# A four-layer transformer block on one core: gates cut into pieces, a context copy moved, and loads tied behind a point of the order

## The chip, the cores and the metric

The kernel runs on one core of one Trainium2 chip. The metric is the device time of one execution, in microseconds. The kernel before takes 3809.88 us, the median of three runs (3807.89 to 3815.07). The profile comes from one further execution, which took 3822.21 us.

## The reference

Eight sequences of 512 tokens by 256 features, with a context of the same shape for each, go through four residual steps. All arithmetic that matters here is in 32-bit floats.

```python
x = x + tanh(g_xattn[0]) * mlstm(layernorm(x), ctx, ctx)     # "cell": 8 heads of 32
x = x + tanh(g_ffn[0])   * attn_and_experts(layernorm(x))    # 32 heads of 8, then experts
x = x + tanh(g_xattn[1]) * cross_attention(ctx, ctx, layernorm(x))  # 16 heads of 16
x = x + tanh(g_ffn[1])   * product_key_experts(layernorm(x)) # top 8 of 4096
```

The part that the change is about is the first line's gates. From query, key and value a small product makes 8 input gates and 8 forget gates for each token. Then, along the 512 tokens of a sequence:

```python
log_f = log_sigmoid(fg)
cs = cumsum(log_f, axis=1)
log_D = cs[:, :, None] - cs[:, None, :] + ig[:, None, :]     # masked above the diagonal
D_mat = exp(log_D - max(log_D, axis=-1))
C = (q k^T / sqrt(32)) * D_mat
h = (C / (max(|sum C|, exp(-max log_D)) + 1e-6)) v
```

The kernel needs of it, for each head and token, the running sum cs and the running maximum of (input gate - cs). Both are scans along the tokens.

## The kernel before, in words

The program has two stages. The attention phase (to about 2850 us of the profile) does the first three residual steps for all sequences. The final stage (L1459 on) does the product-key experts. The change touches only the attention phase.

**The main loop.** Attention is cut into 24 jobs. A job is one sequence's 16 heads: ("A", m, 0) and ("A", m, 1) are the two halves of the self-attention of the m-th sequence in order, ("C", m, 0) is its cross-attention. Each job has 16 steps, and a step has two halves. A job passes through the loop twice. First its maxima: per half step 8 matrix instructions make scores of 128 queries by two heads by 512 keys in PSUM (`sc`, two buffers, L422), and VectorE reduces them to negative maxima (`nm`, L440). Later its exponentials: the scores are made again with the maximum folded in, and ScalarE takes the exponential (`pr`, L469), which then multiplies the values (`av`, L485). In the steady state each half step holds one product of maxima of one job and one product of exponentials of an earlier job. A job starts its maxima when its operands are there (`ready`). If it isn't ready, the loop goes on with the exponentials alone.

**Lanes beside it.** Everything else in the phase is written as Python generators, called lanes, which are stepped between the half steps: `between` (moves operands of A jobs), `values1`, `after`, `before((0, 2, ... 7))` (cell and queries of the sequences but the second), `behind` (experts, then the operands of C jobs), `before((1,))` (cell and queries of the second sequence, in buffers lent by the experts), `contexts` (keys and values of the cross-attention) and `fill` (products for the final stage). A lane yields a number, the TensorE time that it has just used; or ("wait", t), after which it isn't stepped until a nominal clock has advanced by t; or ("rest", event), after which it is stepped once the event has been noted; or ("take", ...), for a PSUM bank. In each half step `beside` (L1353) hands out a credit of TensorE time. It goes through the lanes in a fixed order of preference and steps the first that can run. The two lanes at places 3 and 4 (cells; experts) change places with each turn. Once the first job has begun, the lane of the second sequence stands ahead of both.

**Who sets the order on an engine.** TensorE executes in the order in which the program is traced (`manual_schedule` with PE alone, L1448). On the other engines a planner orders the instructions by its own costs and by their readiness, and it may move an instruction that is ready far ahead of where it was traced. `tc.issue_after(ins)` ties the instructions traced in its block that are on `ins`'s engine behind `ins` in that engine's order. `beside` uses it: VectorE instructions of a lane's step stay behind the newest reduction of maxima.

**The gates.** In `cell` (L713), after the product `gp` (L726), VectorE adds the gates' biases (L735, two instructions on 8 partitions by 512 tokens). ScalarE takes Abs, Exp and Ln (L742 to L744; the last needs another table). VectorE then makes log_sigmoid (L745), the running sum (L746, a scan), the difference (L750), the running maximum (L752, a scan), their sum (L753) and a sign (L754). The result goes to DRAM, from where it is broadcast to all partitions. All of this is traced in one step of the lane.

**The start.** The first sequence's x (`x0`), the gates' weights, its transposed context (`cT0`) and its context (`cx0`) are loaded first. `load_keys` copies the context into a spread layout `cte` (L228, on ScalarE for the first sequence, on GpSimd for later ones). The first cell's weighed sums (L693) read `cte`. After the first cell come the queries: keys and queries are stored to DRAM and loaded back in another layout (`spread`), values (`vk`, L946 and L948) are stored by GpSimd's queue (L953). Then the first job's maxima can begin. `pk` and `vk` share two buffers.

**Loads on GpSimd's queue.** `load` (L526, a sequence's x for the experts), `load_context` (L532), `Tiles.begin` (L565, x and context of the cells from the third sequence on) and the reload of x at L882 are issued from GpSimd. Weights of the experts are too, and do not change. Nothing but readiness ties the former to a place in GpSimd's order.

Of the kernel before, what the change touches and what calls it, by code (L numbers as in the profile page):

```python
# [10 lines left out]
F32 = mybir.dt.float32  # L11
# [4 lines left out]
AF = mybir.ActivationFunctionType  # L16
# [20 lines left out]
def kernel(  # L37
# [142 lines left out]
    def attention_phase(ctx: ExitStack):  # L180
# [39 lines left out]
        cte = cst.tile([P, NC, WC], F32, name="cte")  # L220
        nc.vector.memset(cte, 1.0)

        def load_keys(eng, staged, ce, b, copy):

            eng.dma_start(staged, cx[b].rearrange("(c p) d -> p c d", p=P))
            for c2 in range(2):
                part = slice(2 * c2, 2 * c2 + 2)
                copy(  # L228
                    ce[:, part, : 8 * 33].rearrange("p c (h e) -> p c h e", e=33)[:, :, :, 0:32],
                    staged[:, part].rearrange("p c (h e) -> p c h e", e=32),  # L230
                )

        load_keys(
            nc.sync, trp.tile([P, NC, D], F32, name="cx0", tag="Xa"), cte, order[0], nc.scalar.copy
        )

        gwm = cst.tile([P, 4, 40], F32, name="gwm")
        nc.gpsimd.memset(gwm, 0.0)
# [284 lines left out]
        kds, vcs = {}, {}  # L523
        xbs, lnx, qks, vds, xds, weights = {}, {}, {}, {}, {}, {}

        def load(m):  # L526

            xbs[m] = xbp.tile([P, NC, D + 1], F32, name="X")
            nc.gpsimd.dma_start(xbs[m][:, :, :D], xds[m])
            nc.gpsimd.memset(xbs[m][:, :, D], 1.0)  # L530

        def load_context(m, tag):  # L532
            cT = cxp.tile([P, NK, S], F32, name="cT", tag=tag)
            nc.gpsimd.dma_start(cT, cxT[order[m]].rearrange("(k p) s -> p k s", p=P))
            return cT

        def load_first(n):
# [17 lines left out]
        class Tiles:  # L555
# [9 lines left out]
            def begin(self, m):  # L565

                b = order[m]
                if m == 0:
                    return x0, cT0, cte
                qn = self.tokens("qn")  # L570
                self.loader.dma_start(qn, x[b].rearrange("(c p) d -> p c d", p=P))
                cT, ce = self.context(m)
                load_keys(self.loader, self.stream(), ce, b, nc.gpsimd.tensor_copy)
                return qn, cT, ce

            def context(self, m):
# [136 lines left out]
        def cell(m, own, loaded):  # L713
# [24 lines left out]
            if m == 0:  # L738
                with tc.issue_after(gated.ins):
                    constants()  # L740

            nc.scalar.activation(e, z, AF.Abs)  # L742
            nc.scalar.activation(e, e, AF.Exp, scale=-1.0)
            nc.scalar.activation(e, e, AF.Ln, bias=1.0)  # L744
            nc.vector.scalar_tensor_tensor(z, z, 0.0, e, ALU.min, ALU.subtract)  # L745
            nc.vector.tensor_tensor_scan(  # L746
                cs, ones[:8, 0:1].to_broadcast([8, S]), z, 0.0, ALU.mult, ALU.add
            )

            nc.vector.tensor_tensor(a, a, cs, ALU.subtract)  # L750
            nM = z
            nc.vector.tensor_tensor_scan(nM, a, a, -3.0e38, ALU.max, ALU.max)  # L752
            nc.vector.tensor_tensor(cs, cs, nM, ALU.add)  # L753
            nc.vector.tensor_scalar(nM, nM, -1.0, None, ALU.mult)  # L754
            nM_d = drm.tile([8, S], F32, name="nM_d")
# [123 lines left out]
                if pair == 2:  # L879
                    rested.add(("cell", m))  # L880
            Xa = own.stream()
            nc.gpsimd.dma_start(Xa, x[b].rearrange("(c p) d -> p c d", p=P))  # L882
            if m == 0:
                mu, rs = yield from layernorm(None, hk, "q")
                for c in range(NC):
# [16 lines left out]


        def queries(m, own, Xa):
            xn = own.tokens("xn")


# [34 lines left out]
            for c in range(NC):  # L942
                ps = project(w, nT, c)
                pk = trp.tile([P, S], F32, name="vk", tag="pk", bufs=2)[:, : 32 * 9]
                heads = pk.rearrange("p (h e) -> p h e", e=9)
                nc.gpsimd.memset(heads[:, :, 8], 1.0)  # L946
                for f in range(2):
                    nc.any.tensor_copy(  # L948
                        heads[:, 16 * f : 16 * f + 16, 0:8].rearrange("p (j g) e -> p j g e", g=4),
                        ps.rearrange("p (j f g e) -> p j f g e", f=2, g=4, e=8)[:, :, f],  # L950
                    )

                (nc.sync if m else nc.gpsimd).dma_start(  # L953
                    vds[m][:, :, c], pk.rearrange("p (f n) -> p f n", f=2)
                )
                yield 1.0
# [103 lines left out]
        def contexts():  # L1060

            for half in (range(M // 2), range(M // 2, M)):
                for i in (1, 2):
                    if i == 1 and half[0]:
                        yield ("rest", ("A", 1, 0))
                    w = wsp.tile([P, NK, D], F32, name="wkv", tag="wkv")
                    nc.sync.dma_start(w, w3[i].rearrange("(k p) n -> p k n", p=P))
                    for m in half:
                        cT = load_context(m, "cT")
                        if m == 0 and i == 1:  # L1070
                            yield ("rest", ("begun", 0))
                        yield ("wait", 5)
                        for cost in (keys3, values3)[i - 1](m, w, cT):
                            yield cost
                            yield ("wait", 2)
# [277 lines left out]
        def beside(credit):  # L1353

            nonlocal turn
            while credit > 0:
                turn += 1
                first = lanes[:3] + (lanes[3:5] if turn % 2 else lanes[4:2:-1]) + lanes[5:]
                if ("begun", 0) in rested:
                    first.insert(3, lanes[5])  # L1360
                lane = next((lane for lane in first if lane.runnable()), None)
# [571 lines left out]
```

## Time and profile before

| | before |
|---|---|
| median of three runs | 3809.88 us (3807.89 to 3815.07) |
| profiled execution | 3822.21 us |
| its span, first to last instruction | 3820.4 us |
| PE busy | 3521.1 us, 92% |
| DVE busy | 2246.6 us, 59% |
| ACT busy | 1756.5 us, 46% |
| POOL busy | 600.5 us, 16% |
| mean granted TensorE clock | 0.968 |
| mean DMA traffic | 90 GB/s |

PE is TensorE's matmuls, PEld its weight loads, DVE VectorE, ACT ScalarE, POOL GpSimd, SP SyncE; a "q" behind a name is that engine's queue of DMA issues and waits. L440 is line 440 of the kernel. A group's row gives line, engine, operation and tile as out<-in. In a timeline the two numbers ahead of a row are its start and its busy time, both in us; in brackets stands how long the engine was idle before it and what ended that idleness. "x2" behind a row means that two instructions are merged in it. The row of digits of an engine in the page shows its busy tenths in 40 equal slices of the span, 95.5 us each; PEclk is the granted TensorE clock in tenths of full speed. Of the time around the span, 1.8 us, the profile tells nothing.

### The profile page before, as it was taken

How to read it: one execution, taken by the hardware profiler on the slowest of the kernel's cores; microseconds unless marked ns; L12 is line 12 of the kernel's file. 1: busy time of each engine (PE TensorE's matmuls, PEld its weight loads, DVE VectorE, ACT ScalarE, POOL GpSimd, SP SyncE). 2: the span in 40 equal slices, each digit the busy share in tenths (PEclk: the TensorE clock that was granted, in tenths of full speed). 3: DMA queues.
4: the chain of work that ended last, by engine and by line, in shares of the span. 5: the costliest groups of instructions: out<-in, count | busy, mean ns of one | idle time of the engine just before them, and what ended most of it. 6: DMA issues, size and time to landing. Idle time of an engine off the chain costs nothing.

```text
span 3820.4 us, 76232 instructions
## 1 busy us (share of the span) xinstructions
PE 3521.1 (92%) x31049; PEld 1833.6 (48%) x31049; DVE 2246.6 (59%) x5491; ACT 1756.5 (46%) x2300; POOL 600.5 (16%) x646
## 2 busy tenths in 40 slices
PE   5789888999999999999999999999899999999998
PEld 2333333443444344334433443434346777777777
DVE  4565656556555555545555543544422689999993
ACT  2124454444445444445445444444443455555552
POOL 3122102111101010101200200100000133333331
PEclk7779999999999999999999999999999999999999
DMA  4423212322412332332332242230434433333331
GB/s 128 114 72 85 66 48 79 90 72 63 123 53 81 92 87 80 90 90 68 96 93 59 80 109 87 90 85 23 139 118 149 119 110 107 107 107 107 107 106 38
DMA packets 225195, 345.35 MB, mean 90 GB/s; under 512 B 25982, under 2 KB 173470, under 8 KB 216542
## 3 DMA queue, kind: packets, MB, share of 16 engines
q1 hardware_dynamic: 206796, 277.43, 24.6%
q0 software_dynamic: 16864, 62.46, 5.6%
q8 instruction: 244, 4.00, 0.4%
q10 hardware_dynamic: 1184, 0.58, 0.1%
q14 instruction: 107, 0.88, 0.1%
HBM read 238.50 MB, written 101.09 MB: 89 GB/s over the span
## 4 chain that ended last, share of the span: by engine, by line
PE 78%; DVE 10%; ACT 2%; issue 2%; DMA 1%; POOL 0%; SPq 0%; DVEq 0%; ACTq 0%; POOLq 0%
PE sc L422 22%; PE acc L1775 12%; PE ps_hd L131 10%; PE av L485 7%; DVE nm L440 7%; PE cf L1755 4%; PE ps_y L1039 3%; PE ps_sim L1507 3%; PE ps_q L381 3%; PE ps_h L1020 3%; PE ps_p L370 2%; PE cav L842 2%; PE csc L857 2%; PE ps_hl L131 1%; PE ps_t L351 1%
## 5 line engine op out<-in xcount | busy, mean ns | idle before, releaser
L440 DVE TENSOR_REDUCE nm<-sc 128x2 f32<-128x1024 f32 x768 | 938.9, 1225 | 953.6 <-PE sc L422 952.3
L469 ACT ACTIVATE pr<-sc 128x1024 f32<-128x1024 f32 x768 | 783.0, 1023 | 949.9 <-PE sc L422 949.3
L422 PE MATMUL sc<-ka,qa 32*128 32x512 f32 x3072 | 913.0, 661 | 117.7 <-DVE nm L440 117.3
L422 PE MATMUL sc<-qa,ka 32*128 32x512 f32 x3072 | 864.9, 651 | 20.8 <-ACT pr L469 19.0
L1775 PE MATMUL acc<-up_sb,gs 64*128 64x256 f32 x4096 | 468.4, 382 | 1.3 <-DVE gs L1764 1.3
L422 PEld LDWEIGHTS sc<-ka,qa 32*128 32x128 f32 x3072 | 247.0, 187 | 462.4 <-DVE nm L440 275.0
L131 PE MATMUL ps_hd<-xT,dw 128*64 128x256 f32 x3584 | 432.8, 387 | 15.0 <-DVE pd L862 6.5
L485 PE MATMUL av<-pr,v 128*32 128x512 f32 x3072 | 420.9, 621 | 4.4 <-DMA v<-v_d 4.3
L1775 PEld LDWEIGHTS acc<-up_sb,gs 64*128 64x128 f32 x4096 | 390.0, 187 | 52.4 <-issue 4.7
L131 PEld LDWEIGHTS ps_hd<-xT,dw 128*64 128x64 f32 x3584 | 247.0, 138 | 231.4 <-issue 98.1
L1745 POOL TENSOR_TENSOR m<-o,cwT 128x1024 f32<-128x1024 bf16 x128 | 243.6, 1903 | 584.0 <-DVE o L1743 260.8
L1222 ACT COPY hb<-ps_hd 128x512 f32<-128x512 f32 x224 | 130.9, 585 | 286.3 <-PE ps_hd L131 250.9
L422 PEld LDWEIGHTS sc<-qa,ka 32*128 32x128 f32 x3072 | 233.1, 185 | 59.8 <-ACT pr L469 45.4
L485 PEld LDWEIGHTS av<-pr,v 128*32 128x32 f32 x3072 | 61.1, 109 | 301.6 <-issue 296.1
L835 ACT ACTIVATE pd<-mb,aT 128x512 f32<-128x512 f32 (+1 forms) x224 | 113.6, 553 | 177.1 <-PE cav L842 110.8
L1764 DVE TENSOR_TENSOR gs<-cf,gs 128x1024 f32<-128x1024 f32 x128 | 155.7, 1218 | 42.2 <-PE cf L1755 27.4
L827 POOL TENSOR_SCALAR_AFFINE_SELECT mb<-mb 128x256 f32<-128x256 f32 x112 | 45.4, 406 | 755.9 <-ACT pd L835 436.4
L1755 PE MATMUL cf<-m,m 64*64 64x64 f32 x8192 | 153.2, 222 | 3.1 <-issue 2.3
L1755 PEld LDWEIGHTS cf<-m,m 64*64 64x64 f32 x8192 | 135.3, 135 | 41.2 <-issue 40.8
L1741 ACT CAST m<-o 128x1024 f32<-128x1024 bf16 x128 | 133.7, 1045 | 39.3 <-DVE o L1739 35.5
L1020 PE MATMUL ps_h<-fT,w1e 128*128 128x256 f32 x512 | 135.0, 396 | 7.9 <-DVE o L513 7.2
L1039 PE MATMUL ps_y<-w2e,heT 128*128 128x256 f32 x512 | 130.6, 393 | 2.5 <-issue 1.7
(263 smaller groups left out, 4037.2 us busy)
## 6 DMA issues: line engine op xcount, KB each, us to landing
h_d<-hb SPq DMA_DIRECT2D x224, 256.0 KB
gs<-h_d SPq DMA_DIRECT2D x56, 1024.0 KB
dw<-in_down SPq DMA_DIRECT2D x112, 256.0 KB
w1e<-in_w POOLq DMA_DIRECT2D x16, 1024.0 KB, 5.7
w2e<-in_w POOLq DMA_DIRECT2D x16, 1024.0 KB, 6.5
mb<-nM_d SPq DMA_DIRECT2D x28, 512.0 KB
cT<-in_cxT POOLq DMA_DIRECT2D x22, 512.0 KB, 4.5
qk_d<-pk SPq DMA_DIRECT2D x32, 256.0 KB
```

Of the source, the lines that this page charges most:

```text
L131: nc.tensor.matmul(ps[64 * q : 64 * q + 64, :], dw[:, k, :], runs[:, :, q, :], start=(k == 0), stop=(k == NK - 1),)
L422: nc.tensor.matmul(sc[:, i, :], lhs[r : r + 32, g, c * P : (c + 1) * P], rhs[r : r + 32, g, :], start=True, stop=True,)
L440: newest = nc.vector.tensor_reduce(self.nm[:, c, 2 * half : 2 * half + 2, g], sc, AX.X, ALU.max, negate=True)
L469: nc.scalar.activation(mine[jj], sc, AF.Exp)
L485: nc.tensor.matmul(self.av[32 * j : 32 * j + 32, :], self.va[:, c, h * (self.hd + 1) : h * (self.hd + 1) + 32], pr[j // 2][:, j % 2, :], s ...
L1020: nc.tensor.matmul(ps[:, :D], w1e[:, k, f * P : (f + 1) * P], fT[:, k, i * D : (i + 1) * D], start=(k == 0), stop=(k == NK - 1),)
L1039: nc.tensor.matmul(py[:, c, :], hT[:, f, c * P : (c + 1) * P], w2e[:, f, :], start=(f == 0), stop=(f == NF - 1),)
L1741: nc.scalar.copy(m1, o1)
L1745: nc.gpsimd.tensor_tensor(m2, o2, tokens(cw), ALU.mult)
L1755: nc.tensor.matmul(cf[64 * q : 64 * q + 64, h, s, :], m2[rows, 4 * q + s // 2, :, s % 2], m1[rows, 4 * q + s // 2, :, s % 2], start=True, ...
L1764: nc.vector.tensor_tensor(gv, cf.rearrange("p h s i -> p i h s"), gv, ALU.mult)
L1775: nc.tensor.matmul(accs[n][q], gs[n % 2][rows, i, :], up_sb[rows, i, :], start=(i == 0), stop=(i == 63),)
```

## The change

There are four edits.

1. **Gates.** For all cells but the first, three waits are put into the gates: ("wait", 2) behind ScalarE's third function, ("wait", 1) behind the running sum, ("wait", 1) behind the running maximum. The lane comes back at a later half step after each, so that the chain is traced in four pieces.
2. **First context.** The copies that spread the first context are traced behind the first gates' Abs and tied to ScalarE's order behind it. The load itself stays where it was. `load_keys` becomes `spread_context`, without the load.
3. **GpSimd's loads.** `settled` becomes the last of the four memsets of `vk` in the first sequence's queries. Loads on GpSimd's queue that are traced once it is set (`load`, `load_context`, `Tiles.begin`, the reload of x) are tied behind it. In `contexts`, the first transposed context is loaded behind the wait for the first job's beginning, not ahead of it.
4. **Order of lanes.** The lane of the cells stands ahead of the lane of the experts in three turns of four, where it was one of two.

```diff
-        def load_keys(eng, staged, ce, b, copy):
-
-            eng.dma_start(staged, cx[b].rearrange("(c p) d -> p c d", p=P))
+        def spread_context(ce, staged, copy):
+
             for c2 in range(2):
...
-        load_keys(
-            nc.sync, trp.tile([P, NC, D], F32, name="cx0", tag="Xa"), cte, order[0], nc.scalar.copy
-        )
+        cx0 = trp.tile([P, NC, D], F32, name="cx0", tag="Xa")
+        nc.sync.dma_start(cx0, cx[order[0]].rearrange("(c p) d -> p c d", p=P))
...
+        settled = None
+
+        def behind_first():
+
+            return tc.issue_after(settled.ins) if settled else nullcontext()
+
         def load(m):
             xbs[m] = xbp.tile([P, NC, D + 1], F32, name="X")
-            nc.gpsimd.dma_start(xbs[m][:, :, :D], xds[m])
+            with behind_first():
+                nc.gpsimd.dma_start(xbs[m][:, :, :D], xds[m])
...
         def load_context(m, tag):
             cT = cxp.tile([P, NK, S], F32, name="cT", tag=tag)
-            nc.gpsimd.dma_start(cT, cxT[order[m]].rearrange("(k p) s -> p k s", p=P))
+            with behind_first():
+                nc.gpsimd.dma_start(cT, cxT[order[m]].rearrange("(k p) s -> p k s", p=P))
...
-                self.loader.dma_start(qn, x[b].rearrange("(c p) d -> p c d", p=P))
-                cT, ce = self.context(m)
-                load_keys(self.loader, self.stream(), ce, b, nc.gpsimd.tensor_copy)
+                with behind_first():
+                    self.loader.dma_start(qn, x[b].rearrange("(c p) d -> p c d", p=P))
+                    cT, ce = self.context(m)
+                    staged = self.stream()
+                    self.loader.dma_start(staged, cx[b].rearrange("(c p) d -> p c d", p=P))
+                    spread_context(ce, staged, nc.gpsimd.tensor_copy)
...
-            nc.scalar.activation(e, z, AF.Abs)
+            size = nc.scalar.activation(e, z, AF.Abs)
+            if m == 0:
+                with tc.issue_after(size.ins):
+                    spread_context(cte, cx0, nc.scalar.copy)
             nc.scalar.activation(e, e, AF.Exp, scale=-1.0)
             nc.scalar.activation(e, e, AF.Ln, bias=1.0)
+
+            if m:
+                yield ("wait", 2)
             nc.vector.scalar_tensor_tensor(z, z, 0.0, e, ALU.min, ALU.subtract)
...
+            if m:
+                yield ("wait", 1)
             nc.vector.tensor_tensor(a, a, cs, ALU.subtract)
...
+            if m:
+                yield ("wait", 1)
             nc.vector.tensor_tensor(cs, cs, nM, ALU.add)
...
-            nc.gpsimd.dma_start(Xa, x[b].rearrange("(c p) d -> p c d", p=P))
+            with behind_first():
+                nc.gpsimd.dma_start(Xa, x[b].rearrange("(c p) d -> p c d", p=P))
...
-                nc.gpsimd.memset(heads[:, :, 8], 1.0)
+                last = nc.gpsimd.memset(heads[:, :, 8], 1.0)
+                if m == 0:
+                    settled = last
...
-                        cT = load_context(m, "cT")
                         if m == 0 and i == 1:
                             yield ("rest", ("begun", 0))
+                        cT = load_context(m, "cT")
                         yield ("wait", 5)
...
-                first = lanes[:3] + (lanes[3:5] if turn % 2 else lanes[4:2:-1]) + lanes[5:]
+                first = lanes[:3] + (lanes[3:5] if turn % 4 else lanes[4:2:-1]) + lanes[5:]
```

More of the change, by code (lines that the diff above doesn't have):

```diff
@@ L904, in queries @@
         def queries(m, own, Xa):
+            nonlocal settled
             xn = own.tokens("xn")
```

## The prediction

> **What bounds the kernel now.** I read the page's first two parts first, then stretches of time, then single timelines.
>
> ```profile
> span 3820.4 us, 76232 instructions
> PE 3521.1 (92%) x31049; PEld 1833.6 (48%) x31049; DVE 2246.6 (59%) x5491; ACT 1756.5 (46%) x2300; POOL 600.5 (16%) x646
> PE   5789888999999999999999999999899999999998
> PEclk7779999999999999999999999999999999999999
> ```
>
> PE is the bound, with 299 us of idle. The busy time by stretches says where:
>
> ```profile
> 0.00:110.00 110.00, 55.60 (x237) 28.13 (x237) 43.35 (x105) 26.74 (x52) 37.70 (x60) 0.76 0.44 129
> 110.00:300.00 190.00, 156.10 (x620) 66.58 (x618) 118.01 (x196) 44.94 (x73) 33.27 (x60) 0.77 0.29 84
> 300.00:2850.00 2550.00, 2371.86 (x15638) 1025.75 (x15635) 1350.56 (x2023) 1195.12 (x1451) 280.37 (x393) 0.98 0.29 83
> ```
>
> The columns are the stretch, its length, busy PE, PEld, DVE, ACT and POOL, the granted clock, DMA. PE idles 54 us before the first attention product, 34 us in the next 190, 178 us (7%) in the rest of attention. The change touches attention alone; the final stage (L1459 on) has the same instructions.
>
> Next the gates, one chain for each of eight cells, found by L742. Seven are "later cells", starting at 132.8, 256.1, 512.2, 830.9, 1144.4, 1507.9 and 1892.7 us. DVE in the last one:
>
> ```profile
> 1891.96 1.51 DVE L735 TENSOR_SCALAR pd<-gp,gb_sb 8x512 f32<-8x512 f32 x2
> 1896.46 0.68 DVE L745 SCALAR_TENSOR_TENSOR pd<-pd,mb 8x512 f32<-8x512 f32 x1 [2.99 <-ACT mb L744]
> 1897.17 1.21 DVE L746 TENSOR_TENSOR_SCAN pd<-ones,pd 8x512 f32<-8x512 f32 x1
> 1898.31 1.19 DVE L440 TENSOR_REDUCE nm<-sc 128x2 f32<-128x1024 f32 x1
> 1899.55 1.22 PE L422 MATMUL sc<-ka,qa 32*128 32x512 f32 x1 [4.18 <-DVE nm L440]
> ```
>
> DVE stands 2.99 us at L745 for ScalarE's third function. The maximum (L440), whose product was ready at 1894.4, is queued behind L745 and L746. PE then stands 4.18 us for that maximum's PSUM. This is what the pieces attack.
>
> Last the start, PE and ACT:
>
> ```profile
> 16.00 1.14 ACT L228 COPY cte<-cx 128x512 f32<-128x512 f32 x2 [11.86 <-DMA cx<-in_cx]
> 17.16 1.07 ACT L360 COPY qT<-ps_t 128x512 f32<-128x512 f32 x2
> 17.80 3.64 PE L726 MATMUL gp<-qT,gwm 128*40 128x512 f32 x4 [3.90 <-ACT qT L360]
> 106.18 2.08 PE L381 MATMUL ps_q<-ws,nT 128*128 128x256 f32 x4 [4.89 <-ACT vk L948]
> 108.18 2.09 PE L422 MATMUL sc<-ka,qa 32*128 32x512 f32 x8
> ```
>
> The transposes end at 13.90, but qT's copy stands behind a copy that waits for a context load nobody needs until 46 us. At 106.18 PE waits for the value copies, which wait for stores (v_d at 99.72 landed at 105.46, 5.7 us; the ones at 111.49 and 114.94 took 2.3).
>
> **The Trainium skill.** "TensorE: Matmul & The Clock Gate", "Part 1: The HAM clock gate", says that after about 3.4 us of idleness the array falls to half rate until a busy window. The trace agrees: the 128x512 product (L422) takes 587 ns at least and 1218 at most, and the record of the granted clock has half-rate stretches at 1897.8 (6.8 us) and 1522.3 (3.4 us), beside gates. Its section "Architectural detail" calls VectorE and ScalarE strict FIFO; L440 behind L745 shows it. "ScalarE: Activation LUTs", "What ACT_TABLE_LOAD costs", gives 1283 ns; the rows of L744 have 1283, but no 1380 ns drain behind it. "DMA: Bandwidth & Descriptors", "Issuing engines are not separate DMA queues": loads from any engine share 16 DMA engines. The 5.7 against 2.3 us above fits.
>
> **The change part by part.** The sums are made against the profiled execution, 3822.2 us (span 3820.4 plus 1.8 around it). The runs' median, 3809.9, is 12.3 lower; I subtract the gain from it unscaled.
>
> *Gates in pieces.* Nothing is added on DVE: per later cell two L735 (0.74 each), then 0.68 + 1.21 | 0.68 + 1.21 | 0.68 + 0.41 = 4.87 us, now as three DVE pieces behind ScalarE's, each traced after at least one further half step's maximum. I listed PE's gaps over 1 us from 2 us before each L742 to 1.5 us after its L754. Those ended by a maximum or a copy that stood behind L745 to L754 are 2.99 + 1.43, 4.12 + 2.73, none, 1.03, 1.08, 2.36 and 4.18: 19.9 us. Others stay: 1.35 us behind L735 at 512, and 1.80 + 2.58 + 1.53 us ended by ACT's L469, since three functions and two table loads (3 x 0.63 + 2 x 1.28 = 4.45 us) still stand in one row on ACT. If the split were perfect: -19.9. A piece of 1.89 us and a maximum of 1.23 together fill a half step of about 3.3 us (a job's 32 maxima take some 105 us), so other DVE work is pushed and a third may come back. I take -13, between 0 (DVE full anyway) and -20.
>
> *Clock.* Two half-rate stretches after 300 us lie at such a gap (3.4 + 6.8 us) and three before it (13.7 at 139.9, 3.4 at 262.8, 3.4 at 269.6): 30.7 us, half of which is lost, 15. They need the gap to go fully, and the early ones have other idleness beside them: -4, between 0 and -15.
>
> *The gates' latency.* The waits of 2, 1 and 1 make three half steps, about 10 us, of a chain that now takes 8.6 to 14.6 from L742's start to L754's end; each cell's end may come up to 5 us later. Behind it are its queries and its attention job. At A(7,0) that job is late already: maxima stop for 19.0 us (2217.7 to 2236.7), but with 0.7 us of PE idle, because fillers cover it. Cover gone, it costs what A(7,1)'s gap costs: 24.5 us with 4.9 idle. The lane order now lets the cells go first in three turns of four, not two. I set both together at 0, from -5 to +8.
>
> *First context.* The two copies (0.57 each) leave qT's way. First copy then at about 12.8, first gate product at 13.4 instead of 17.8: 4.4 us, if its context has landed (no wait is seen at 20.4; I assume by 16.7). The copies reappear between Abs and Exp: +1.14. Net -3.2; bounds 0 to -4.4. POOL's load L882 waits for these copies (17.44, then about 23); behind it stand a b2e scaling and a memset, and the next needed POOL instruction is L647 at 39.97, so that costs nothing.
>
> *POOL loads behind the first values.* Moved behind the fourth L946 (113.80): the contexts' first cT (5.92), the second cell's cT (67.57), qn (84.98), cx (85.82) and x (92.47), and X (86.57): six issues of about 0.8 us, 512 KB each. Four issued at 85 to 92.5 land by 98.1, over the q and k stores and the weight load. Removed, I expect the k store's landing (93.96 to 98.5) at 2.3 and the first v_d at 3.5 instead of 5.7: 2.2 + 2.2 = -4.4 at the first maximum. Against it, PE's order keeps the contexts' product (114.80) 6.6 us after the first score product, and its cT is now issued after the fourth memset (now 5.6 us after), plus 0.8 to issue and 4.5 to land (median of 22, most 9.0): it is ready 10.9 us after, so PE stands 4.3. With faster stores the memset comes earlier: 3, of which other waits there (PE idles 18.0 us in the first job's 105) absorb some. I take +3 for it with the burst of 3 MB behind. SP's queue holds v0's load and the second half's spreads at that time (117 to 121); half-two scores start only at about 217, so these have cover. POOL's first LayerNorm operation behind it (118.30) may slip 1 us. Start and loads: -3.2 - 4.4 + 3 = about -4.6, call it -4; from -9 to +4.
>
> Sum: -13 - 4 + 0 - 4 = -21. 3822.2 becomes 3801, and the median 3809.9 becomes 3789.
>
> **Rivals.**
> *The stalls move.* DVE and ACT are only shifted: PE meets the same delays in smaller pieces, because ACT's 4.45 us block stays and each piece makes the next maximum late. Against: DVE was idle 1.6 to 6 us in each gate. Then gates give -4, clock 0, start -4: 3802; with the start lost also, 3808.
> *All of it.* Gaps -20, clock -12, start -8: 3770. Against: some ACT gaps sit in the same places.
> *Slower: jobs come late.* With the lanes' order, experts and operands (the lane behind C jobs) go first in one turn of four. C(0,0) already has the longest early pause, 7.1 us (668.2 to 675.3). A missed start makes the loop run one-sided; the two such places with cost (2336.8 to 2361.2, 2671.7 to 2696.9) have 4.9 and 4.6 us of PE idle, 4.8 a place. From five new such places (24 us) the gain of 21 is gone; at eight, 3809.9 - 21 + 38 = 3827. Against: the other pauses between jobs up to A(6,1) are 1.5 to 4.9 us, so most operands are early.
> *No effect of the order on POOL*, if the planner would have put these loads late anyway, can't be: the trace shows four at 85 to 92.
>
> **How the numbers follow.** A comparison of this kernel tells 0.2%, 7.6 us, from nothing. Forecast, 0.45: 3789, own range 3780 to 3800. All of it, 0.12: 3770. Stalls move, 0.20: 3802 to 3808, of which 0.04 falls under 3802. Jobs late, 0.23: 3812 to 3830, three quarters of it above 3817.5. With half of the second case and a quarter of the last left out, 0.88 would remain; the forecast's own tails take it to about eight in ten between 3770 and 3818. Faster: 0.45 + 0.12 + 0.04 = 0.61; same 0.16 + 0.06 = 0.22; slower 0.17.
>
> **What would show it.** Right: an L440 between L746 and L750 and between L752 and L753 at every later gate; DVE's idle before the third function's reader (10.9 us, 6 times) gone; PE gaps by L440 at the seven gates under 7 us in all; first gate product near 13.5, first maximum near 103 rather than 110.4; a PE wait for the contexts' cT of 2 to 5 us. Wrong: PE idle from 300 to 2850 not below 178 us, new pauses before C(0,0) or other jobs over 7 us, or a first maximum after 108.

## The result, and the profile after

The changed kernel takes 3795.21 us, the median of 15 runs (3783.34 to 3806.91); the kernel before, run beside it, 3815.24 us (15 runs, 3805.05 to 3824.56). The ratio is 0.995, 95% interval 0.9936 to 0.9963. The gain of 20 us is what was forecast (21), to within what can be measured. The forecast of 3789 us was taken off the earlier median of 3809.9.

The first parts of the page of the changed kernel:

```profile
span 3787.1 us, 76231 instructions
PE 3495.5 (92%) x31049; PEld 1827.5 (48%) x31049; DVE 2244.9 (59%) x5490; ACT 1755.2 (46%) x2300; POOL 601.5 (16%) x646
PE   5789888998999999999999999998899999999998
PEclk7889989999999999999999999999999999999999
```

Its stretches, with bounds moved to the same points of the work (the first maximum, 200 us on, the end of attention):

```profile
0.00:101.00 101.00, 50.27 (x233) 26.13 (x233) 43.18 (x105) 26.63 (x52) 33.07 (x51) 0.77 0.38 109
101.00:290.00 189.00, 153.31 (x672) 65.86 (x676) 120.31 (x200) 49.55 (x76) 39.96 (x72) 0.83 0.37 108
290.00:2830.00 2540.00, 2366.57 (x15662) 1028.91 (x15656) 1346.72 (x2019) 1194.53 (x1454) 279.33 (x390) 0.99 0.29 84
```

TensorE's idle time is 291.6 us in all, 299.3 before: 50.7, 35.7 and 173.4 us in the three stretches against 54.4, 33.9 and 178.1, and 31.7 against 32.9 in the final stage. So the two profiled executions, 33.3 us apart, differ by only 8 us of idleness. The other 25.6 us are busy time of the same 31049 matmuls. The record of the granted clock has 189.7 us at half rate after and 246.7 before, and the matmuls inside those stretches, at twice their time, lost 69 us after and 97 before: 28 us, a little more than the whole difference in busy time.

One execution's clock is partly chance, so each run's was used. The record knows only full and half rate; with a mean clock c in a run of t us, the time at half rate is 2(1 - c)t, and t less half of that is "the rest": about what the run would take at full rate (about, because some of the time at half rate is idle, and nothing is lost there: in the profiled executions the matmuls lost 0.36 to 0.40 us per us at half rate, not 0.5). Over the 15 runs of the change the mean time at half rate is 214 us and the rest 3689.6 us. The clocks of the 15 runs of the kernel before aren't on record; 27 other runs of it, those beside e1 to e4 below, have 228 and 3700.6. Of 18 us between these means, 7 are clock and 11 the rest, so far as two groups of runs can be compared: the rest of the kernel before differs by 3 us from group to group.

VectorE in the last gate after the change (L752 to L757 are ScalarE's functions, L439 the maxima, L761 to L774 the gate):

```profile
1846.44 1.20 DVE L439 TENSOR_REDUCE nm<-sc 128x2 f32<-128x1024 f32 x1
1852.57 1.23 DVE L439 TENSOR_REDUCE nm<-sc 128x2 f32<-128x1024 f32 x1 [4.93 <-PE sc L421]
...
1854.36 0.67 DVE L761 SCALAR_TENSOR_TENSOR pd<-pd,mb 8x512 f32<-8x512 f32 x1
1855.06 1.21 DVE L762 TENSOR_TENSOR_SCAN pd<-ones,pd 8x512 f32<-8x512 f32 x1
1856.20 1.19 DVE L439 TENSOR_REDUCE nm<-sc 128x2 f32<-128x1024 f32 x1
...
1859.68 1.21 DVE L439 TENSOR_REDUCE nm<-sc 128x2 f32<-128x1024 f32 x1
1860.81 1.73 DVE L773 TENSOR_TENSOR pd<-pd 8x512 f32<-8x512 f32 x1
```

At this gate VectorE no longer waits for ScalarE's third function: a maximum comes before L761, one behind each scan. (At two of the seven later gates it still waits, 1.40 us at 264.81 and 3.27 us at 514.27.) But the 4.93 us ahead of the second maximum are a new wait for scores, and TensorE's own rows of that gate say where it comes from:

```profile
1851.40 0.69 PE L421 MATMUL sc<-qa,ka 32*128 32x512 f32 x1 [1.81 <-ACT pr L468]
1860.94 0.69 PE L421 MATMUL sc<-ka,qa 32*128 32x512 f32 x1 [0.81 <-DVE nm L439]
```

The gap of 4.18 us behind L440 has become 0.81 + 0.52 (the latter at 1864.18), and 1.81 us behind ScalarE's exponential stands beside it. Counted so at the seven later gates, TensorE's gaps behind a maximum or copy that the gate holds up fell from 19.9 to 7.1 us (3.09 + 0.47, 0.54, none, none, none, 1.70, 0.81 + 0.52; those from 0.4 us up are counted, and before there were none between 0.4 and 1 us). The gaps ended by ScalarE's exponential rose from 5.9 to 12.1 us (2.58, 4.45, 1.76, 1.48, 1.81). The longest has a cause of its own. ScalarE at the third later gate:

```profile
509.30 0.63 ACT L756 ACTIVATE mb<-mb 8x512 f32<-8x512 f32 x1
509.94 1.28 ACT L1057 ACT_TABLE_LOAD   x1
511.24 1.06 ACT L1057 ACTIVATE heT<-heT 128x1024 f32<-128x1024 f32 x1
512.31 1.28 ACT L757 ACT_TABLE_LOAD   x1
513.61 0.63 ACT L757 ACTIVATE mb<-mb 8x512 f32<-8x512 f32 x1
```

An expert's activation (L1057) has slipped between Exp and Ln, with a table load of its own: 6.9 us from L752 (508.64) to the exponential's turn (515.55) instead of 4.5. VectorE waits for it too:

```profile
514.27 0.68 DVE L761 SCALAR_TENSOR_TENSOR pd<-pd,mb 8x512 f32<-8x512 f32 x1 [3.27 <-ACT mb L757]
```

The start, rows of TensorE:

```profile
13.67 3.49 PE L736 MATMUL gp<-qT,gwm 128*40 128x512 f32 x4
...
98.86 2.08 PE L380 MATMUL ps_q<-ws,nT 128*128 128x256 f32 x4 [7.07 <-ACT vk L972]
...
110.13 2.47 PE L369 MATMUL ps_p<-cT,wkv 128*128 128x256 f32 x5 [3.28 <-issue]
```

The first gate product is 4.1 us earlier (17.80 before), the first maximum 7.6 us (102.8 against 110.4), and TensorE stands 3.28 us until 110.13 (the row names no releaser, but the contexts' load landed at 110.04). Yet the second cell's gate starts at 133.3 us, where it was at 132.8 before. GpSimd's rows say why:

```profile
116.90 1.16 POOL L227 COPY cte<-Xa 128x512 f32<-128x512 f32 x2 [6.40 <-DMA Xa<-in_cx]
...
119.18 0.23 POOL L103 TENSOR_SCALAR ln_rs<-ln_mv 128x4 f32<-128x4 f32 x1
```

The third sequence's context is now loaded late (issued at 108.85, landed 116.84), and its copy stands in GpSimd's order ahead of the second sequence's LayerNorm. GpSimd waits 6.40 us for it. In the kernel before the same operation had a free way:

```profile
118.30 0.23 POOL L103 TENSOR_SCALAR ln_rs<-ln_mv 128x4 f32<-128x4 f32 x1 [2.68 <-DVE ln_mv L102]
```

With 7.6 us gained ahead of it, it should have come at about 110.7 by this estimate, and the LayerNorm's statistics (L102) were in fact ready at 110.2; it came at 119.2. At the second cell's gate the gain of the start is gone. Whether that is what it costs the kernel is asked with e6 and e8 below.

### The profile page after: what moved, and what is told of

Its sections match the earlier page's. It is cut to its first block, busy times and chain, and to the rows that moved or that the text cites. A ratio compares the mean times of both kernels' runs of the same rounds, so it can differ in the third digit from the quotient of the medians.

```text
span 3787.1 us, 76231 instructions
## 1 busy us (share of the span) xinstructions
PE 3495.5 (92%) x31049; PEld 1827.5 (48%) x31049; DVE 2244.9 (59%) x5490; ACT 1755.2 (46%) x2300; POOL 601.5 (16%) x646
## 3 DMA queue, kind: packets, MB, share of 16 engines
q1 hardware_dynamic: 206796, 277.43, 24.5%
## 4 chain that ended last, share of the span: by engine, by line
PE 66%; DVE 7%; ACT 2%; DMA 1%; issue 1%; SPq 0%; DVEq 0%; ACTq 0%
PE sc L421 16%; PE acc L1799 12%; PE ps_hd L131 11%; PE av L484 6%; DVE nm L439 5%; PE cf L1779 4%; PE ps_sim L1531 3%; PE ps_y L1063 2%; PE ps_h L1044 2%; PE ps_q L380 2%; PE ps_p L369 1%; PE ps_hl L131 1%; PE cav L862 1%; PE csc L877 1%; PE ps_g L1180 1%
## 5 line engine op out<-in xcount | busy, mean ns | idle before, releaser
L439 DVE TENSOR_REDUCE nm<-sc 128x2 f32<-128x1024 f32 x768 | 939.0, 1225 | 926.2 <-PE sc L421 924.2
L1765 ACT CAST m<-o 128x1024 f32<-128x1024 bf16 x128 | 133.7, 1045 | 39.5 <-DVE o L1763 35.7
```

The lines of the kernel that those rows point to most:

```text
L439: newest = nc.vector.tensor_reduce(self.nm[:, c, 2 * half : 2 * half + 2, g], sc, AX.X, ALU.max, negate=True)
L1765: nc.scalar.copy(m1, o1)
```

## The experiments

All ran beside the kernel before, in three groups on one chip each (before: 3813.28, 3815.88 and 3814.13 us, 27, 26 and 50 runs). None leaves out any of the computation. "Half rate" and "rest" are means over the runs, worked out as above; the rest of single runs of one kernel scatters by 2 to 4 us. Before has 228 and 3700.6 in the first group (e1 to e4), 236 and 3698.2 in the second (e5 to e8), 233 and 3697.5 in the third (e9 to e12).

| run | median us | ratio to before | 95% interval | half rate us | rest us |
|---|---|---|---|---|---|
| the change | 3795.2 | 0.995 | 0.9936 to 0.9963 | 214 | 3689.6 |
| e1 gates alone | 3817.0 | 1.0006 | 0.9994 to 1.0019 | 186 | 3723.7 |
| e2 lanes alone | 3839.6 | 1.0049 | 1.0031 to 1.0068 | 261 | 3705.0 |
| e3 loads alone | 3814.2 | 0.9999 | 0.9986 to 1.0011 | 230 | 3700.7 |
| e4 gates and lanes | 3796.4 | 0.9944 | 0.9929 to 0.9959 | 213 | 3690.4 |
| e5 early gates | 3818.6 | 1.0005 | 0.9993 to 1.0017 | 222 | 3707.5 |
| e6 third loads later | 3796.4 | 0.9947 | 0.9927 to 0.9967 | 222 | 3687.1 |
| e7 cells always first | 3814.0 | 0.9994 | 0.9982 to 1.0006 | 228 | 3699.1 |
| e8 without load order | 3792.1 | 0.9942 | 0.992 to 0.9963 | 216 | 3684.7 |
| e9 gates, shorter wait | 3832.9 | 1.006 | 1.0038 to 1.0082 | 240 | 3712.7 |
| e10 another wait | 3813.6 | 1.0002 | 0.999 to 1.0015 | 241 | 3693.7 |
| e11 early gates and lanes | 3799.1 | 0.9968 | 0.9956 to 0.998 | 224 | 3689.2 |
| e12 two turns of three | 3808.9 | 0.9991 | 0.998 to 1.0003 | 228 | 3694.7 |

**The parts one by one.** e1 is the kernel before with the three waits in the gates of all cells but the first:

```diff
             nc.scalar.activation(e, e, AF.Ln, bias=1.0)
+            if m:
+                yield ("wait", 2)
...
+            if m:
+                yield ("wait", 1)
```

> The kernel before with the three waits in the later gates alone. Theory 'the gates are the gain': 15 to 19 us faster (the forecast's -13 and -4), an L440 between the scans at every later gate, no DVE idle behind ScalarE's third function. Rival 'the gates need the lanes' order': without it every later cell ends some 5 us later, A(7,0) starts later than the 19.0 us pause of before, and the kernel gains less than 8 us. Rival 'the gain is the start': within 4 us of before.

e2 is the kernel before with the lanes' order alone:

```diff
-                first = lanes[:3] + (lanes[3:5] if turn % 2 else lanes[4:2:-1]) + lanes[5:]
+                first = lanes[:3] + (lanes[3:5] if turn % 4 else lanes[4:2:-1]) + lanes[5:]
```

> The kernel before with the cells' lane first in three turns of four alone. Forecast's step: 0 (from -5 to +8), the pause ahead of A(7,0) shorter than 19.0 us. Rival 'lanes make C jobs late': 5 us or more slower, with a pause over 7.1 us ahead of C(0,0). Rival 'the order of the lanes is the gain': 10 us or more faster.

e3 ties GpSimd's loads behind the fourth memset, with the first context's copies left where they were:

```diff
+            with behind_first():
                 nc.gpsimd.dma_start(cT, cxT[order[m]].rearrange("(k p) s -> p k s", p=P))
```

> The kernel before with GpSimd's loads behind the fourth memset of the first values, and the contexts' first load behind the job's beginning, alone. Forecast's step: first maximum 4.4 us earlier than 110.4, PE then waits 3 us for the contexts' cT: 1 us faster, from -4 to +5. From the changed kernel's trace I now expect the first maximum at most 2 us earlier (its first v_d store took 7.0 us to land, with no load beside it), and POOL's LayerNorm operation of the second cell late by up to 8 us: 0 to 6 us slower. Theory 'loads are a loss': slower by 3 or more.

e4 has the waits of e1 and the line of e2 together, and nothing of the start.

> The kernel before with the pieces in the gates and the lanes' new order, but neither edit of the start. Theory 'the gates are the gain': as fast as the gates alone, 15 to 19 us faster. Rival 'the two need each other': gates alone gain under 8, both together 15 or more. Rival 'the gain is the start': within 4 us of before.

Alone the pieces give nothing, the lanes cost 19 us (0.49%), the loads give nothing; pieces and lanes together give the whole gain, 0.56%. So the parts can't be added: in these four orders pieces and lanes gain only together, and the start is worth nothing that shows. (What the change has over e4 is the start: 3689.6 against 3690.4 in the rest, 0.8 us.) e3 also moves the contexts' first load behind the first job's beginning, as the change does. Its first maximum comes at 102.0 us, 8.4 us earlier than before, where at most 2 were expected, and its time doesn't move.

Nor do the gates' stalls tell the fast kernels from the slow. Counted alike at the seven later gates (every gap of TensorE from 0.4 us up that VectorE or ScalarE ends, the 1.35 us behind the biases included), they are 27.2 us before and 19.2 in the change. But they are 19.3 in e1, 23.6 in e9, 17.4 in e7, 20.0 in e10 and 19.9 in e12 too, which gain next to nothing or lose.

e1's profile says what happens to the pieces alone. At the end of the maxima of A(5,1) it is 35 us ahead of the kernel before (1850.2 against 1884.8 us). Then VectorE's maxima stop, here between two jobs:

```profile
1848.99 1.23 DVE L440 TENSOR_REDUCE nm<-sc 128x2 f32<-128x1024 f32 x1 [0.39 <-PE sc L422]
...
1923.80 1.23 DVE L440 TENSOR_REDUCE nm<-sc 128x2 f32<-128x1024 f32 x1 [0.68 <-PE sc L422]
```

Some 74 us without a maximum, and 51.6 us more ahead of A(7,0): in this loop that means that those jobs' operands aren't ready. That the gates, which now end later after their start, make them late is argued, not shown; e9 below takes it up. The loop goes on with exponentials and fillers, but TensorE idles 14.3 us up to the end of A(6,0), 7.9 in A(7,0) and 21.8 in C(5,0), where it had 8.8, 5.6 and 6.4 before. e1 has by far the least time at half rate (186 us) and the longest rest: it gains 21 us on the clock and loses 23 in the rest. The three places above have 23 us more idleness, but the whole execution has only 12.6 more (312.0 against 299.4), so lateness is a part of that loss, and what else is in it is open.

With the lanes' order, in the changed kernel, the pauses ahead of A(6,0) and A(7,0) are 2.9 and 4.4 us. A(7,1) then waits 42.1 us (24.5 before), with 10.6 us of idleness.

**Which gates.** e5 has the pieces in the gates of the cells 1 to 4 alone, e11 the same with the lanes' order of the change (cells first in three turns of four; the expectation below says one):

```diff
+            if 0 < m < 5:
+                yield ("wait", 2)
```

> The kernel before with the pieces in the gates of the second to fifth cell alone, the last three cells' gates whole, lanes as before. Theory 'the pieces lose by late cells': the pauses of 73.6 and 51.6 us ahead of A(6,0) and A(7,0), which the gates alone showed, are gone or halved, and what they cost with them: 10 to 20 us faster than before. Rival 'pieces are worth nothing without the lanes, whatever comes late': within 4 us of before, like the gates alone.

> The kernel before with pieces in the gates of the cells m = 1 to 4 alone and the lanes' order of the change (cells first in one turn of four). The three late gates stay whole. Theory (the lanes' order alone loses because a whole gate then falls between jobs that have no cover for it): the time lies between that of the lanes alone, 19 us above before, and of pieces and lanes together, 18 us below it, so within 12 us of before. Rival: the early gates are what the lanes' order needs, and the full gain of 16 to 20 us comes. Second rival: it is as slow as the lanes alone, 15 to 20 us above before, and the late gates decide.

e5 is like e1: no gain, with pauses of 11.6 us ahead of A(6,0) and 44.5 ahead of A(7,0). e11 brings 15 us by the medians and 12 by the ratio, with 8 to 17 us in its interval: it lies between the theory (within 12 us) and the first rival (16 to 20), and only the second rival, a loss as with the lanes alone, is out. So pieces in the early gates are enough to turn the loss into most of the gain. What the three late gates in pieces add is the difference between e4 and e11: 0.24% or 9 us by the ratios, whose intervals overlap a little, and 5 us by the means, each less that of its own kernel before. One of e11's late gates, whole, on VectorE:

```profile
1484.68 1.21 DVE L748 TENSOR_TENSOR_SCAN pd<-ones,pd 8x512 f32<-8x512 f32 x1
1485.93 0.68 DVE L754 TENSOR_TENSOR pd<-pd 8x512 f32<-8x512 f32 x1
1486.54 1.21 DVE L440 TENSOR_REDUCE nm<-sc 128x2 f32<-128x1024 f32 x1
```

The maximum stands behind three of the gate's operations (the one before these rows is L747), with none between the first scan and the difference, and TensorE waits 3.16 us for it there (at 1487.80). So a stall of the kind that the pieces remove is there, in a kernel that is nearly as quick.

**Is it the wait or the order?** e9 is e1 with the nominal wait behind each later gate cut from 9 to 4:

```diff
-            yield ("wait", 9)
+            yield ("wait", 4 if m else 9)
```

> The kernel before with the gates in pieces alone, lanes as before, and the wait of nominal length behind each later cell's gate cut from 9 to 4, so that the values' part of a cell is ordered nearer to its gate. Theory (the pieces lose their gain because the cells' later parts are ordered too late, so that attention jobs wait for states): the pauses ahead of the jobs A(6,0) and A(7,0), 73.6 and 51.6 us with the gates alone, shrink below 30 us each and the time falls to 3800 to 3806, some 10 us below before. Rival (lateness is of the order itself, not of this wait): within 4 us of before. Second rival: the values' part then stands at the head of TensorE's and VectorE's queues before its inputs are there, and it is 5 to 20 us slower than before.

The pause ahead of A(6,0) is gone (2.6 us), and the time is 19 us over before. The pause has moved to A(7,0):

```profile
2213.37 1.23 DVE L440 TENSOR_REDUCE nm<-sc 128x2 f32<-128x1024 f32 x1 [1.44 <-PE sc L422]
2279.84 1.23 DVE L440 TENSOR_REDUCE nm<-sc 128x2 f32<-128x1024 f32 x1 [0.68 <-PE sc L422]
```

66.5 us from one maximum to the next, with 13.4 us of TensorE's idleness up to that job's end and 12.5 in C(5,0). It is the second rival by its size, but what that names as cause doesn't show on TensorE: its first product behind the shortened wait (`at`) stands waiting at none of the seven later gates. That a job is late is shown; that this wait makes it late isn't.

**The order of lanes.** e7 is the change with the cells first in every turn. e12 is e8 (the change without the order of the loads, below) with the cells ahead of the experts (its expectation says the maxima) in two turns of three, that is `turn % 3`. e7's edit:

```diff
-                first = lanes[:3] + (lanes[3:5] if turn % 4 else lanes[4:2:-1]) + lanes[5:]
+                first = lanes[:3] + lanes[3:5] + lanes[5:]
```

> The changed kernel with the cells' lane ahead of the experts' in every turn. Theory 'the order serves to make up for the pieces' latency, and three in four does so': within 5 us of the changed kernel. Rival 'the more the cells lead the better': 5 us or more faster than it. Rival 'experts and C jobs come late': slower by 5 us or more, with a pause over 7 us ahead of a C job.

> The changed kernel without the order of the loads, with the cells' lane ahead of the maxima in two turns of three in place of three of four. Theory (the share matters only in that neither kind of job is always late): within 5 us of that kernel, so 3788 to 3797 beside a before of 3815. Rival: the exact order of single jobs decides more than the share, and it is 5 to 20 us slower. A gain of 5 us or more would say that three of four is too many.

e7 loses the gain, as its second rival has it: C(0,0) waits 16.4 us (3.1 in the change) and C(3,0) 25.4 (4.9), jobs whose operands come from the lane that now goes last. TensorE's idleness to the end of these jobs is 8.9 and 9.0 us, where the change has 9.0 and 4.8: the late jobs cost nothing in one place and 4.2 us in the other, too little for the loss. Over the whole run e7's rest is 9.5 us above the change's and its clock costs 7 more.

e12 is 17 us slower than e8, from which it differs in one digit: its rival, that the exact order of single jobs decides, fits. The digit changes the share too, from three in four to two in three, so that the share plays no part isn't shown. No pause between its jobs up to A(7,0) is over 7.0 us. Its profile has 12.7 us more idleness (293.3 against 280.6), in pieces of 1 to 4 us over some ten jobs, with no one place to point at.

**The start.** e6 ties the third sequence's loads and its copy on GpSimd behind the second sequence's LayerNorm. e8 takes the order of the loads out of the change:

```diff
-            return tc.issue_after(settled.ins) if settled else nullcontext()
+            return nullcontext()
...
+                        cT = load_context(m, "cT")
                         if m == 0 and i == 1:
                             yield ("rest", ("begun", 0))
-                        cT = load_context(m, "cT")
```

> The changed kernel, the third sequence's loads and its context's copy on GpSimd moved behind the power of the second sequence's first LayerNorm. Theory 'in the changed kernel that copy holds GpSimd, and with it the LayerNorm': this power starts near 112 instead of 119.5, the second cell's gates near 126 instead of 133.3, and the kernel is 3 to 8 us faster than the changed one. Rival 'an earlier start is given back in the first job whatever is done': the gates come earlier, but the time stays within 2 us of the changed kernel's.

> The changed kernel without the order of GpSimd's loads (they may run early again, the contexts' first load too). Theory 'the loads' order is worth nothing here': within 3 us of the changed kernel, the first maximum at 104 to 107 and the second sequence's LayerNorm not held up. Rival 'the loads' order is a part of the gain': 5 us or more slower than the changed kernel.

Both mend the slip. The LayerNorm's row in e8:

```profile
112.86 0.23 POOL L103 TENSOR_SCALAR ln_rs<-ln_mv 128x4 f32<-128x4 f32 x1 [2.21 <-DVE ln_mv L102]
```

It comes at 112.08 in e6 and 112.86 in e8, for 119.18 in the change, and the second cell's gate at 129.4 and 126.3 instead of 133.3. The time of e6 stays (rest 2.5 us lower, time at half rate 8 us longer), as its rival has it. e8 has the lowest rest of all (3684.7), 5 us under the change, but the rest of the kernel before alone differs by half of that between two groups, and its interval holds the change's ratio. So 4 to 7 us at 130 us are worth nothing that shows at the end; that the load order costs a few isn't shown.

**ScalarE's row.** e10 is e8 with one more turn of other work between Exp and Ln, meant to split the row that now ends the longest gaps:

```diff
             nc.scalar.activation(e, e, AF.Exp, scale=-1.0)
+            if m:
+                yield ("wait", 1)
             nc.scalar.activation(e, e, AF.Ln, bias=1.0)
```

> The changed kernel without the order of the loads, with one more piece: a turn of other work between the gate's Exp and its Ln on ScalarE. Theory (the pieces left ScalarE's own row, 4.45 us of functions and table loads without a break, as the gates' longest stall, and TensorE's gaps ended by ScalarE's copies of the probabilities at the gates grew from 5.9 to 12.1 us): these gaps halve and the time is 3 to 6 us below the same kernel without this piece, so 3786 to 3789 beside a before of 3815. Rival: one turn more makes the cells later still, and it is 3 to 15 us slower than that kernel. Second rival: within 3 us of it.

It is 21 us slower than e8 (with kernels before that differ by 1.8 us), and it doesn't test its theory. ScalarE at the third later gate:

```profile
531.23 0.63 ACT L756 ACTIVATE mb<-mb 8x512 f32<-8x512 f32 x1
531.87 1.28 ACT L759 ACT_TABLE_LOAD   x1
533.17 0.63 ACT L759 ACTIVATE mb<-mb 8x512 f32<-8x512 f32 x1
```

Exp and Ln stand together as before, here and at five of the other six gates; one has a copy of 0.56 us between. No exponential came in. So e10 shows what one more turn does to the order of everything behind it, without doing what it was for. Its page (span 3816.7 us):

```profile
PE 3533.4 (93%) x31049; PEld 1838.6 (48%) x31049; DVE 2238.3 (59%) x5475; ACT 1764.1 (46%) x2316; POOL 603.9 (16%) x646
...
PEclk7789999998999999999999999999999999999999
```

And that of e8 (span 3786.0 us):

```profile
PE 3505.2 (93%) x31049; PEld 1831.8 (48%) x31049; DVE 2245.5 (59%) x5490; ACT 1754.9 (46%) x2300; POOL 601.7 (16%) x646
...
PEclk7889989999999999999999999999999999999999
```

TensorE's idleness is nearly the same, 283.3 against 280.8 us (span less busy time). The 30.7 us between the spans are 28.2 us of busy time; the time at half rate is 258 against 210 us, and the matmuls inside it lost 104 against 81, 23 us more. Over all runs, too, e10 is at half rate for 25 us longer, and its rest is 9 us longer.

## Why the prediction was right, and where it wasn't

The total was right, 20 for 21 us, but its parts didn't come to it in the way that was forecast. By its own steps:

**Gates, -13 us.** Right in size: -12.8 by the same count. A maximum stands between the second scan and the sum (L770 and L773) at all seven gates, and between the first scan and the difference (L762 and L768) at six; not at 133.3, which kept its 3.09 us. The sign asked for under 7 us, and 7.1 were left; VectorE's wait for the third function, which was to go, stayed at two gates. Wrong was "Others stay": gaps ended by ScalarE grew by 6.2 us. Half of the rival in which the stalls move was true, for the reason it gave (ScalarE's row stays whole), and an expert's activation inside a row made one of them 4.45 us. The net at the gates is 6.6 us. And this step takes a stall less at a gate for as much less time of the kernel, which the runs don't bear out: e1, e7, e10 and e12 have shortened the gates as much or nearly, and have next to no gain.

**Clock, -4 us.** Under-sized: about -7 on the means of the runs, and -28 in the profiled pair. The step priced the clock from two stretches of one execution; over the runs it is a mean, and two single profiles can't check it.

**Latency and lanes, 0 together.** The sum came out near it, and this step hides most of what happened. The forecast put the two at 0 as small effects that cancel. They are large: pieces without the lanes' order lose all of their gain, with A jobs late (e1), the lanes' order without pieces costs 19 us (e2), and neither sign was forecast for one alone. Why the lanes alone lose is only partly known: 16 us are clock (261 us at half rate against 228) and the rest is 4 us longer, while long pauses between jobs are no more than before (38.9 us ahead of A(7,1), 25.5 ahead of C(7,0), 6.0 or less elsewhere). e11 shows that with four early gates in pieces the loss is gone, no more.

**Start, -4 us.** Wrong: 0. The first gate product (13.67, forecast 13.4), the first maximum (102.8, forecast near 103) and the wait for the contexts' load (3.28, forecast "PE stands 4.3", taken as 3) are right. The composition isn't. The key store's landing did fall, from 4.5 to 2.7 us (forecast 2.3). But the first store of values took 7.0 us to land (91.19 to 98.14), where 3.5 was forecast with GpSimd's loads gone and 5.7 was measured with them. The wrong neighbour was blamed: in the kernel before, those loads had landed by 98.1, and the store was issued at 99.72. What ran beside it was SyncE's queue, with the weights and the spreads of keys. While the first store was under way, that queue's packets took 39% of the 16 engines' time before, 51% in the change, 38% in e8 and 52% in e3, and the store took 5.7, 7.0, 5.3 and 7.3 us; the stores of 2.3 us had nothing beside them. "DMA: Bandwidth & Descriptors", "Issuing engines are not separate DMA queues", in the Trainium skill, says that transfers from all engines share 16 DMA engines, and these figures agree, though no run moved SyncE's transfers alone. e3's expectation, "with no load beside it", misreads this too.

The other step that failed is "POOL's first LayerNorm operation behind it (118.30) may slip 1 us". It came at 119.2 where an earlier start promised 110.7: 8 us, because the copy L227, which waits for a load, is in that queue too and was not counted among what is moved. "TensorE: Matmul & The Clock Gate", "Architectural detail", calls GpSimd strict FIFO on each of its own processors; the 6.40 us at L227 with a ready LayerNorm behind agree. But this slip isn't why the start is worth nothing: e6 mends it and is no faster, and e3's first maximum is 8.4 us earlier for no gain. What was wrong is that time gained at the start is time gained at the end; where it goes is open.

**Jobs late, the slower rival.** Its mechanism is real, its place and price were not. In the change itself C(0,0) waits less than before (3.1 against 7.1 us), and the pause that grew is A(7,1)'s, 42.1 us with 4.0 us more idleness. By the forecast's own list a new pause over 7 us would have shown it wrong; this one was paid for in part by A(7,0)'s, which fell from 19.0 to 4.4 us with 1.5 us less idleness. Where the C jobs do come late (e7) a place costs nothing or 4.2 us, below the 4.8 that the forecast charged.

**Slips in its figures.** They change nothing: with the start lost too, the rival in which the stalls move comes to 3806 us (3809.9 - 4), not 3808, and a gate's chain took up to 15.1 us (1144.37 to 1159.46), not 14.6.

How firm is a right total? e10 and e12 stand one turn and one digit from e8, and lie 21 and 17 us behind it; e7 stands as near to the change and has none of its gain. The profile of the kernel before says nothing of which of such orders the change would meet. The gates' stalls that the forecast counted are shown; that the whole came to -20 and not to 0 or -5 depended on the order that these edits happened to make, and in that the right total is luck. The same scatter is a rival to the account of e1, e2 and e4: that pieces and lanes need each other for a reason, and aren't, with the kernel before, four orders of which one happened to be good, no run here shows.

## What to carry to other kernels

Where lanes share one order, an edit that adds or moves a yield changes the place of everything behind it: try it with its neighbours (one turn more, one digit of the share) before giving a gain of half a per cent to the mechanism, since here neighbours were 17 to 21 us apart. Count with a load that is tied later also what waits for its data on the same in-order queue, and ask what stands behind that. Before loads are moved out of a slow store's way, see in the trace whose transfers are beside it. And compare idle time, time at half rate and the rest separately: two kernels whose profiles had the same idleness were 21 us apart.

## What the runs showed of the hardware that wasn't expected

The scatter between runs goes with the time at half rate. Over 50 runs of the kernel before, on one chip, it goes from 190 to 268 us and the time from 3796.35 to 3827.63, with a correlation of 0.89 and 0.41 us more per us at half rate, which is about what the matmuls lost per such us in the profiled executions (0.36 to 0.40). In the traces, half-rate stretches after 300 us come in multiples of 3.4 us, but for the one that the end of the program cuts. "TensorE: Matmul & The Clock Gate", "Part 1: The HAM clock gate", in the Trainium skill, gives a free-running window of 3413 ns, which agrees, and an idle window of that length for the fall. A whole idle window isn't needed here. The forecast saw the trace agree, though one of the two stretches that it names (1522.3) stands beside a gap of only 2.36 us. In the changed kernel the stretches at 576.7, 597.2 and 1160.3 us (3.4 us each) have no gap over 1.12, 1.08 and 0.62 us in the 3.4 us ahead of them. Of its 53 gaps over 1 us after 300 us, 14 had a stretch at half rate within 3.4 us, and one of 3.1 us had none. What share of idleness in a window is enough, the runs don't tell. The matmuls of the profiled executions lost 61 us (e1) to 104 us (e10) at half rate, 1.6 to 2.7% of the span.
